# Layer 1 of an LSTM-then-quantum-convolution kernel: results of chunks that lie in the ring go to whole buffers and out from there, and later rows are loaded into the ring

## The chip, the cores and the metric

The kernel runs on one core of a Trainium2 chip. The metric is the device time of one execution in microseconds (us), the median of several. Engines are called as in the profile: PE (TensorE), DVE (VectorE), ACT (ScalarE), POOL (GpSimd), SP (SyncE, which here only issues DMAs). DMAs that SP issues are on queue q1 in the profile, those that POOL issues on q0; all run on the core's 16 DMA engines.

## What is computed

The input is x of 16 images x 128 channels x 64 x 64, in fp32. Two layers, each with a group normalization in front and its result added to x:

```
x = x + diagonal_lstm(group_norm(x))      # layer 0: a scan over 127 diagonals, w_is, w_ss
x = x + quantum_conv(group_norm(x))       # layer 1
...
quantum_conv, for every pixel:
    xq = x[:, pixel] @ pre_w.T + pre_b                     # 128 channels -> 4 angles
    z  = expectation values of a 4-qubit circuit of cos, sin(pi/2 * xq)
    out = z @ post_w.T + post_b                            # 4 -> 128 channels
```

Layer 1 needs the mean and variance of layer 0's whole result, and so begins only when layer 0 is done.

## The kernel before

**Where the data lie.** An image is 128 channels (the partitions) x 4096 pixels, 2 MB. The SBUF tile `ring` (line 109) holds 40 of an image's 64 rows, for all 16 images, as 10 blocks of 4 rows: `ring[P, 10, 16, 256]`. One block of one image is 256 floats, 1 KB in each partition, and the next block of the same image lies 16 KB further on. The other 24 rows, the low ones, have gone to the DRAM tensor `low` (line 112) in the course of layer 0.

**Layer 1** (lines 933 to 1109) works in chunks of 8 rows (`CHUNK`, 512 pixels): 8 chunks an image, of which chunks 0 to 2 (`NT` = 3) are low rows and chunks 3 to 7 are in the ring. A ring chunk is two blocks, so a tensor of three dimensions [128, 2, 256] whose runs are 1 KB; a chunk in a tile of its own is [128, 512] with runs of 2 KB. The low chunks need places in SBUF: `places` (line 944) is first a list of 14 whole tiles, the 8 of `spare` and 6 named `low`. `load(n)` (line 947) takes up to n places from the front of the list and puts the next low chunks of the 48 there, in order of images; the first 8 were loaded by SP at the end of layer 0, all later ones are DMAs issued by POOL (`low_rows`, line 857). `rows_of(b, k)` (line 956) gives chunk k of image b wherever it lies.

For an image there are these steps:
- `angles` (line 971): 8 matmuls, one a chunk, into one PSUM bank (line 976).
- `sines` (line 986): ACT adds the offset (991), DVE takes off whole turns (993, 994), ACT takes the sine (996).
- `squares` (line 998): 2 matmuls (1005) and two squares on ACT (1018).
- `outputs` (line 1020): for each half image h, 4 matmuls (1027) into 4 of 5 PSUM banks, one for each chunk.
- `finish` (line 1037): for each chunk one DVE instruction that adds the bank, a bias and x and writes the sum over x in place (line 1046), then a DMA of it to the output on SP (line 1047); then the place is appended to `places`, so that a later low chunk can be loaded there. Such a load has to wait for the DMA out of the place.

**The order** is written out by hand (`tc.manual_schedule`, lines 1058 to 1109). Image 0 is done in half chunks (argument c is 0 or 1). Then, for image b: outputs of half 0, the first part of the sines of image b+2, finish of half 0, `load(3)`, sine, squares of image b+1, outputs of half 1, finish of half 1, `load(2)`, angles of image b+3. Behind image 0's halves stand `load(3)` (line 1084) and `load(2)` (line 1092). Every engine executes its instructions in this order; so SP's DMAs are in the order of the chunks, and POOL's loads in the order of the low chunks.

Of the kernel before, what the change touches and what calls it, by code (L numbers as in the profile page):

```python
# [11 lines left out]
F32 = mybir.dt.float32  # L12
AF = mybir.ActivationFunctionType
ALU = mybir.AluOpType
PSUM = bass.MemoryType.PSUM

P = 128
NB = 16
NH = 64
# [5 lines left out]
ROWS = 4  # L25
BLOCK = ROWS * NW
CHUNK = 2 * BLOCK
# [53 lines left out]
def kernel(  # L81
# [16 lines left out]
    nc = tc.nc  # L98
# [13 lines left out]
    low = dram.tile([NB, P, NLOW * NW], F32, name="low")  # L112
# [13 lines left out]
    spare = [const.tile([P, CHUNK], F32, name=f"spare{i}") for i in range(8)]  # L126
# [6 lines left out]
    b_out = const.tile([P, 1], F32, name="b_out")  # L133

    def block(r):

        return (r + AHEAD if r < SLOTS else r - SLOTS) // ROWS
# [18 lines left out]
    with ExitStack() as scan:  # L156
# [58 lines left out]
        with ExitStack() as prep:  # L215
# [47 lines left out]
            for i in range(2):  # L263
                nc.scalar.dma_start(out=ws_n[i], in_=ws_v[:, 2 * i : 2 * i + 2])
            nc.scalar.dma_start(
                out=qw, in_=q_weights.rearrange("l w a -> (l w a)").partition_broadcast(P)
# [88 lines left out]
            for i in range(2):  # L355
                v = ws_n[i]
# [500 lines left out]
        def low_rows(queue, n, v):  # L857
            b, k = n // NT, n % NT
            of = low[b, :, k * CHUNK : (k + 1) * CHUNK]
            queue.dma_start(out=v, in_=of if len(v.shape) == 2 else of.rearrange("p (k n) -> p k n", n=BLOCK))  # L860
# [4 lines left out]
        with tc.manual_schedule():  # L865
# [26 lines left out]
            v = ring[:, block(NH - ROWS)].rearrange("p i (r w) -> p i r w", w=NW)[:, :, :, NW - STRIP :]  # L892
# [4 lines left out]
            for i, u in enumerate((d, sq)):  # L897
                u = u.rearrange("p i r w -> p i (r w)")
# [34 lines left out]
    lowp = ctx.enter_context(tc.tile_pool(name="lowp", bufs=1))  # L933
# [7 lines left out]
    ths, turns, sqs = {}, {}, {}  # L941


    places = list(spare) + [lowp.tile([P, CHUNK], F32, name=f"low{i}") for i in range(6)]
    lows = []

    def load(n):

        while n and places and len(lows) < NT * NB:
            v = places.pop(0)  # L950
            lows.append(v)
            if len(lows) > 8:
                low_rows(nc.gpsimd, len(lows) - 1, v)
            n -= 1

    def rows_of(b, k):
        if k < NT:
            return lows[NT * b + k]
        q = block(2 * ROWS * k)
        return ring[:, q : q + 2, b, :]  # L960

    def half(v, c):

        if c is None:
            return v
        return v[:, c] if len(v.shape) == 3 else v[:, c * BLOCK : (c + 1) * BLOCK]

    def bank(pool, name):
        return pool.tile([P, CHUNK], F32, name=name, tag=pool.name)

    def angles(b, c=None, all_of=None):
        th = half(bank(ps_t, f"theta{b}_{c}") if all_of is None else all_of, c)
        for h in range(2):

            for j in (2, 3, 1, 0):
                nc.tensor.matmul(  # L976
                    th[32 * j : 32 * j + 32, :],
                    lhsT=w_image[:, b, 16 - 16 * h : 48 - 16 * h],
                    rhs=half(rows_of(b, 2 * j + h), c),
                    start=(h == 0),  # L980
                    stop=(h == 1),
                    tile_position=(0, 32 * j),
                )
        ths[b, c] = th

    def sines(b, c=None):

        if b not in turns:
            turns[b] = sinp.tile([P, CHUNK], F32, name=f"y{b}", tag="y")
        y = half(turns[b], c)  # L990
        nc.scalar.activation(y, ths[b, c], AF.Identity, bias=b_image[:, b : b + 1])  # L991
        near = half(nearp.tile([P, CHUNK], F32, name=f"near{b}_{c}", tag="near"), c)
        nc.vector.tensor_scalar(near, y, ROUND, ROUND, ALU.add, ALU.subtract)
        nc.vector.tensor_sub(y, y, near)  # L994
        yield
        nc.scalar.activation(y, y, AF.Sin, scale=TWO_PI)

    def squares(b, c=None):
        ams = []
        y = half(turns[b], c)  # L1000
        for h in range(2):
            am = half(ps_a.tile([P, CHUNK], F32, name=f"am{b}_{h}_{c}", tag=f"am{h}"), c)

            k = 64 * h
            nc.tensor.matmul(  # L1005
                am,
                lhsT=w_amp[k : k + 64, h, :],
                rhs=y[k : k + 64, :],
                start=True,
                stop=True,  # L1010
                tile_position=(k, 0),
            )
            ams.append(am)

        if b not in sqs:
            sqs[b] = [sqp.tile([P, CHUNK], F32, name=f"sq{b}", tag="sq"), turns[b]]
        for am, v in zip(ams, sqs[b]):
            nc.scalar.activation(half(v, c), am, AF.Square)

    def outputs(b, h, c=None):  # L1020
        po = [
            half(bank(ps_o, f"po{b}_{h}_{j}_{c}"), c)
            for j in range(4)
        ]
        for j in range(4):
            k = 32 * j
            nc.tensor.matmul(  # L1027
                po[j],
                lhsT=w_out[k : k + 32, :],
                rhs=half(sqs[b][h], c)[k : k + 32, :],  # L1030
                start=True,
                stop=True,
                tile_position=(k, 0),
            )
        return po

    def finish(b, h, po, c=None):
        for j in range(4):
            k = 4 * h + j
            v = rows_of(b, k)  # L1040
            x1, y, o = half(v, c), po[j], ov[b, :, k * CHUNK : (k + 1) * CHUNK]
            if c is not None:
                o = o[:, c * BLOCK : (c + 1) * BLOCK]
            elif len(v.shape) == 3:
                y, o = (u.rearrange("p (k n) -> p k n", n=BLOCK) for u in (y, o))
            nc.vector.scalar_tensor_tensor(x1, y, b_out, x1, ALU.add, ALU.add)  # L1046
            nc.sync.dma_start(out=o, in_=x1)
            if c != 0:
                places.append(v)

    def idle():

        ps = bank(ps_t, nc.get_next_instruction_name())
        v = w_image.rearrange("p b k -> p (b k)")[:, 0:CHUNK]
        for _ in range(2):
            nc.tensor.matmul(ps, lhsT=w_out, rhs=v, start=True, stop=True)  # L1056

    with tc.manual_schedule():
        load(len(places))

        angles(0, 0)
        angles(0, 1, bank(ps_o, "theta0"))
        first = [sines(0, c) for c in range(2)]
        for later in first:
            next(later)

        th = bank(ps_t, "theta1")
        angles(1, 0, th)
        for later in first:
            next(later, None)  # L1070
        squares(0, 0)
        angles(1, 1, th)
        ths[1, None] = th
        po = outputs(0, 0, 0)
        finish(0, 0, po, 0)
        squares(0, 1)
        later = sines(1)
        next(later)
        po = outputs(0, 1, 0)
        finish(0, 1, po, 0)  # L1080
        next(later, None)
        po = outputs(0, 0, 1)
        finish(0, 0, po, 1)
        load(3)
        angles(2)
        later = sines(2)
        next(later)
        po = outputs(0, 1, 1)
        squares(1)
        next(later, None)  # L1090
        finish(0, 1, po, 1)
        load(2)
        angles(3)
        for b in range(1, NB):
            po = outputs(b, 0)
            later = sines(b + 2) if b + 2 < NB else iter(())
            finish(b, 0, po)
            load(3)
            next(later, None)
            if b + 1 < NB:  # L1100
                squares(b + 1)
            next(later, None)
            po = outputs(b, 1)
            finish(b, 1, po)
            load(2)
            if b + 3 < NB:
                angles(b + 3)
            elif b < NB - 1:
                idle()
# [37 lines left out]
```

## Time and profile before

| | |
|---|---|
| median of 3 runs | 1420.79 us (1420.56 to 1421.28) |
| the profiled execution | 1419.29 us |
| its span, first to last instruction | 1417.5 us |
| busy: PE, DVE, POOL, ACT | 95%, 69%, 65%, 55% of the span |
| last instructions of layer 0, first angle matmuls of layer 1 | 1288.3 us after the span's start |
| first result of image 1 on DVE; last result of image 15 | 1305.6; ends at 1399.5 us |
| DVE for a result chunk (line 1046) | 743 ns, one every 0.66 us |
| an image on PE and on DVE, in the middle of layer 1 | 6.33 us |
| DMAs of results of 256 KB: out of ring places, spare, low tiles | 95, 13, 12 |
| loads of low chunks by POOL: to ring places, spare, low tiles | 20, 8, 12 (6 of them first loads) |

The page cuts the span in 40 slices of 35.4 us; its rows give the busy tenths of each engine and of the DMA engines, and the GB/s moved, slice by slice. The other views take a stretch in us from the span's start. In a line of DMA issues the last number is the median time from issue to landing. The DMA share in a table of stretches is the sum of the packets' times over 16 engines' time; packets overlap a little, so that a full stretch has 1.02 to 1.09. Issues on SP are counted as no engine's busy time.

### The profile page before, as it was taken

To read this page: it belongs to the slowest core of one execution; us is meant where nothing else is said; L and a number is where in the kernel's file an instruction comes from. 1 tells how busy PE (TensorE), PEld (TensorE's weight loads), DVE (VectorE), ACT (ScalarE), POOL (GpSimd) and SP (SyncE) were. 2 spreads that over 40 slices of the span, in tenths; PEclk is the share of its full clock that TensorE was granted. 3 is DMA by queue.
4 is the path that set the end of the run, shared out by engine and by line. 5 is a ranking of instruction groups with operands and counts; after the bars stand their busy time and mean duration, and the time that the engine had idled before them with its cause. 6 is when DMAs were issued, how large, how long until landed. Compare 5 with 4: busy or idle time off the path is not lost. (4 is left out here: it accounts for less than half of the span.)

```text
span 1417.5 us, 20294 instructions
## 1 busy us (share of the span) xinstructions
PE 1351.7 (95%) x6030; PEld 962.8 (68%) x6030; DVE 980.5 (69%) x2549; ACT 778.3 (55%) x1860; POOL 923.4 (65%) x1823
## 2 busy tenths in 40 slices
PE   6778999999999999999999999999999999989994
PEld 5658887777777677667777667777777788785331
DVE  7993565566665666787777776766665567867994
ACT  4655666555555555555555555555555556644330
POOL 4226787777766667788888766777777677763400
PEclk9999999999999999999999999999999999999997
DMA  9980000000000000133333100000000000005999
GB/s 325 366 284 2 1 2 0 1 1 1 1 0 1 0 1 1 60 119 119 119 119 119 60 1 1 0 1 1 1 1 0 1 1 0 11 22 193 390 371 323
DMA packets 91086, 107.06 MB, mean 76 GB/s; under 512 B 5552, under 2 KB 78032, under 8 KB 90976
## 3 DMA queue, kind: packets, MB, share of 16 engines
q1 hardware_dynamic: 86336, 94.39, 19.7%
q0 software_dynamic: 3408, 10.58, 2.0%
q8 instruction: 48, 0.79, 0.2%
q10 hardware_dynamic: 1232, 0.80, 0.2%
q14 instruction: 62, 0.51, 0.1%
HBM read 59.61 MB, written 46.14 MB: 75 GB/s over the span
## 5 line engine op out<-in xcount | busy, mean ns | idle before, releaser
L583 PE MATMUL ps<-spare,wxT 128*128 128x512 f32 (+18 forms) x1280 | 479.7, 518 | 0.7 <-POOL spare L574 0.7
L767 DVE TENSOR_TENSOR ps<-ps,both 128x256 f32<-128x256 f32 (+9 forms) x544 | 221.5, 408 | 305.2 <-PE ps L752 303.8
L771 ACT ACTIVATE ps<-ps,bias 128x512 f32<-128x512 f32 (+23 forms) x480 | 279.3, 583 | 220.3 <-DVE ps L767 183.7
L752 PE MATMUL ps<-spare,w1T 128*128 128x256 f32 (+16 forms) x1272 | 345.9, 354 | 9.8 <-DVE spare L729 4.9
L583 PEld LDWEIGHTS ps<-spare,wxT 128*128 128x128 f32 x1280 | 231.1, 190 | 173.1 <-issue 155.4
L752 PE MATMUL ps<-spare,w0T 128*128 128x256 f32 (+16 forms) x1272 | 344.0, 352 | 0.8 <-POOL spare L608 0.8
L802 ACT COPY both<-ps 128x256 f32<-128x256 f32 (+9 forms) x544 | 191.4, 354 | 181.1 <-PE ps L752 161.5
L617 POOL TENSOR_TENSOR ring<-ring,spare 128x256 f32<-128x256 f32 (+8 forms) x487 | 247.3, 538 | 31.3 <-DVE stats L705 21.2
L752 PEld LDWEIGHTS ps<-spare,w1T 128*128 128x128 f32 x1272 | 230.0, 190 | 35.5 <-DVE spare L834 7.6
L752 PEld LDWEIGHTS ps<-spare,wsT 128*128 128x128 f32 x1088 | 195.1, 190 | 86.1 <-DVE spare L834 34.6
L752 PE MATMUL ps<-spare,wsT 128*128 128x256 f32 (+14 forms) x1088 | 241.3, 365 | 5.3 <-DVE spare L834 3.6
L752 PEld LDWEIGHTS ps<-spare,w0T 128*128 128x128 f32 x1272 | 230.5, 190 | 22.0 <-POOL spare L608 0.9
L574 POOL TENSOR_TENSOR spare<-spare,rstd 128x512 f32<-128x512 f32 (+10 forms) x160 | 170.8, 1067 | 14.8 <-DVE rstd L153 2.3
L569 POOL TENSOR_TENSOR spare<-ring 128x256 f32<-128x256 f32 (+8 forms) x213 | 146.8, 699 | 0.0
L828 ACT ACTIVATE g<-cst 128x256 f32<-128x256 f32 (+20 forms) x320 | 103.0, 368 | 64.3 <-DVE cst L827 63.7
L834 DVE TENSOR_TENSOR spare<-g,ps 128x256 f32<-128x256 f32 (+17 forms) x319 | 105.4, 368 | 43.8 <-ACT g L828 41.9
L564 POOL TENSOR_TENSOR spare<-ring,mean 128x16 f32<-128x16 f32 (+8 forms) x247 | 130.6, 538 | 6.6 <-DVE mean L143 6.4
L608 POOL TENSOR_TENSOR spare<-spare 128x240 f32<-128x240 f32 (+9 forms) x136 | 102.6, 754 | 29.7 <-DVE spare L834 25.8
L771 ACT ACTIVATE g<-ps,bias 128x512 f32<-128x512 f32 (+20 forms) x160 | 97.3, 608 | 27.1 <-DVE ps L767 21.1
L854 POOL COPY spare<-spare 128x16 f32<-128x16 f32 x64 | 21.0, 329 | 134.6 <-DVE spare L834 134.6
L827 DVE TENSOR_TENSOR cst<-cst,ps 128x256 f32<-128x256 f32 (+20 forms) x320 | 104.5, 368 | 5.5
L824 DVE TENSOR_TENSOR ps<-ps,g 128x512 f32<-128x512 f32 (+20 forms) x160 | 95.0, 594 | 17.0 <-ACT g L771 16.6
(368 smaller groups left out, 1099.7 us busy)
## 6 DMA issues: line engine op xcount, KB each, us to landing
out_dram<-ring SPq DMA_DIRECT2D x95, 256.0 KB, 3.6
ring<-in_x_dram SPq DMA_DIRECT2D x80, 256.0 KB, 5.6
low<-ring SPq DMA_DIRECT2D x6, 2048.0 KB, 7.5
ring<-in_x_dram SPq DMA_DIRECT2D x6, 2048.0 KB, 8.3
spare<-in_x_dram SPq DMA_DIRECT2D x27, 256.0 KB, 5.5
rest<-in_x_dram SPq DMA_DIRECT2D x21, 256.0 KB, 5.6
ring<-low POOLq DMA_DIRECT2D x20, 256.0 KB, 6.6
out_dram<-spare SPq DMA_DIRECT2D x13, 256.0 KB, 4.0
```

Source lines behind the costliest of these rows:

```text
L564: nc.gpsimd.tensor_sub(by_pairs(xn, 0, j, n), x0, over(mean1, n))
L569: nc.gpsimd.tensor_sub(by_pairs(xn, 1, j, n), lower, of)
L574: nc.gpsimd.tensor_mul(v, v, r)
L583: nc.tensor.matmul(ps[g][:, :, a:b], lhsT=wxT[:, g * 128 : (g + 1) * 128], rhs=xns[t % 2][:, :, a:b], start=t > 0, stop=True, skip_group_c ...
L617: engine.tensor_add(x1, x1, by_pairs(new, q, j, n))
L752: nc.tensor.matmul(out, lhsT=w[:, g * 128 : (g + 1) * 128], rhs=rhs, start=False, stop=True, skip_group_check=True,)
L767: nc.vector.tensor_add(v, v, both[g][:, a:b])
L771: nc.scalar.activation(to[:, :, a:w], ps[g][:, :, a:w], FUNC[g], bias=bias[:, g : g + 1])
L802: nc.scalar.copy(both[g][:, a:b], ps[g][:, 0, a:b])
L827: nc.vector.tensor_add(c[:, q], c[:, q], ig[:, q])
L828: nc.scalar.activation(th[:, q, a:w], c[:, q], AF.Tanh)
L834: nc.vector.tensor_mul(new[:, q, a:v], th[:, q, a:v], act[GO][:, q, a:v])
```

## The change

There are now two lists. `buffers` has the 14 whole tiles; `places` is empty at first, and gets ring places. The first `load` fills all 14 buffers, every later one takes from `places` alone.

```
-    places = list(spare) + [lowp.tile([P, CHUNK], F32, name=f"low{i}") for i in range(6)]
-    lows = []
-
-    def load(n):
+
+    buffers = list(spare) + [lowp.tile([P, CHUNK], F32, name=f"low{i}") for i in range(6)]
+    places, lows = [], []
+
+    def load(n, places=places):
...
             x1, y, o = half(v, c), po[j], ov[b, :, k * CHUNK : (k + 1) * CHUNK]
+            to, short = x1, len(v.shape) == 3
             if c is not None:
                 o = o[:, c * BLOCK : (c + 1) * BLOCK]
-            elif len(v.shape) == 3:
-                y, o = (u.rearrange("p (k n) -> p k n", n=BLOCK) for u in (y, o))
-            nc.vector.scalar_tensor_tensor(x1, y, b_out, x1, ALU.add, ALU.add)
-            nc.sync.dma_start(out=o, in_=x1)
+            elif short:
+                y = y.rearrange("p (k n) -> p k n", n=BLOCK)
+
+                if len(buffers) > NH // ROWS // 2 - 2:
+                    v = buffers.pop(0)
+                    to = v.rearrange("p (k n) -> p k n", n=BLOCK)
+                    places.append(x1)
+                    short = False
+                else:
+                    o = o.rearrange("p (k n) -> p k n", n=BLOCK)
+            nc.vector.scalar_tensor_tensor(to, y, b_out, x1, ALU.add, ALU.add)
+            nc.sync.dma_start(out=o, in_=v if c is None else to)
             if c != 0:
-                places.append(v)
+                (places if short else buffers).append(v)
...
-        load(len(places))
+        load(len(buffers), buffers)
```

In `finish`, a whole chunk that lies in the ring (`short`) is handled in a new way when more than 6 buffers are free: the sum is written to the buffer at the front of the list, the DMA to the output reads the buffer with runs of 2 KB, the ring place is appended to `places` and the buffer to the end of `buffers`. With 6 or fewer free buffers it is written in place and goes out in runs of 1 KB as before. A low chunk in a whole tile is written in place, and its tile then joins `buffers`. A low chunk that was loaded to a ring place is handled like any other ring chunk. Image 0's half chunks are written in place as before. The number of instructions on DVE and of DMAs doesn't change.

## The prediction

> **What bounds the kernel now.** I read the page's slices first, then the chain of waits, then tables by stage, then the DMA view of two stretches. The page (busy tenths and GB/s in 40 slices of 35.4 us):
>
> ```profile
> DVE  7993565566665666787777776766665567867994
> ...
> DMA  9980000000000000133333100000000000005999
> GB/s 325 366 284 2 1 2 0 1 1 1 1 0 1 0 1 1 60 119 119 119 119 119 60 1 1 0 1 1 1 1 0 1 1 0 11 22 193 390 371 323
> ```
>
> Layer 1 is the last four slices; only there are VectorE and the DMA engines both full. Nothing else is touched by the diff, so the question is which of the two sets the end. The chain of waits for 1240 to 1418 ends like this (start, length, what):
>
> ```profile
> 1396.22 1.32 DVE ring L1046 x2
> 1397.53 0.66 DVEq L1143
> 1398.19 1.32 DVE ring L1046 x2
> ```
>
> VectorE's last result is written at 1399.5. The span ends at 1417.5; so 18 us behind the last computation only transfers run. The list for the output tensor gives the last DMA out of the ring at 1412.7, and in this stretch an issue lands after 3.5 us: 1416.2, then 1.3 us of closing. The DMA view of 1306 to 1350 and of 1350 to 1418 (packets, MB, share of 16 engines; then issues):
>
> ```profile
> q1 hardware_dynamic: 7601, 8.80, 56.0%
> q0 software_dynamic: 2498, 8.18, 48.0%
> ...
> out_dram<-ring SPq DMA_DIRECT2D x23, 256.0 KB, 9.1
> ring<-low POOLq DMA_DIRECT2D x19, 256.0 KB, 6.6
> out_dram<-spare SPq DMA_DIRECT2D x8, 256.0 KB, 8.7
> out_dram<-low SPq DMA_DIRECT2D x6, 256.0 KB, 9.5
> ```
>
> ```profile
> DMA packets 22382, 23.23 MB, mean 342 GB/s; under 512 B 1429, under 2 KB 20718, under 8 KB 22376
> ...
> q1 hardware_dynamic: 22365, 23.14, 99.3%
> ```
>
> From 1306 on the 16 engines are never free: first refills (q0) and results (q1) together, then results alone, nearly all in 1 KB packets. By 1350 SP has issued 23 + 8 + 6 = 37 results of images 1 to 15. VectorE, which the chain shows at 6.33 us an image (8 chunks, 0.79 us each) from 1305.6, has written 56. With about 8 of the 37 still in flight (9 us to land, one about every 1.2 us), VectorE leads by some 27 chunks. **The end is set by transfers**, not by VectorE.
>
> **The change, part by part.** (1) *Runs.* Of the 120 chunks of images 1 to 15, 95 go out of ring places now and 25 out of whole tiles (13 spare, 12 low). After it, the five ring chunks of image 1 still go in place (6 free buffers, and the test wants over 6); from image 2 on every chunk goes from a whole tile. So 90 chunks change from 256 x 1 KB to 128 x 2 KB packets. The price of each, from stretches of the table (PE, PEld, DVE, ACT, POOL; last three: clock, DMA share, GB/s):
>
> ```profile
> 1324.00:1328.00 4.00, 4.00 (x24) 1.35 (x22) 3.97 (x8) 1.25 (x3) 2.86 (x5) 1.00 1.08 397
> ...
> 1340.00:1342.00 2.00, 2.00 (x19) 0.42 (x16) 1.97 (x4) 0.69 (x2) 1.73 (x3) 1.00 1.06 413
> 1352.00:1362.00 10.00, 10.00 (x66) 3.17 (x60) 9.93 (x17) 4.30 (x8) 0.00 (x0) 1.00 1.09 381
> ...
> 1378.00:1382.00 4.00, 4.00 (x26) 1.14 (x24) 3.96 (x7) 1.34 (x3) 0.00 (x0) 1.00 1.03 372
> 1382.00:1390.00 8.00, 8.00 (x32) 2.84 (x34) 7.97 (x14) 2.11 (x4) 0.00 (x0) 1.00 1.03 343
> 1400.00:1408.00 8.00, 0.00 (x0) 0.00 (x0) 0.00 (x0) 0.00 (x0) 0.00 (x0) 0.50 1.03 341
> 1410.00:1412.00 2.00, 0.00 (x0) 0.00 (x0) 0.00 (x0) 0.00 (x0) 0.00 (x0) 0.50 1.03 363
> ```
>
> 1382 to 1390 and 1400 to 1408 are pure 1 KB: 342 GB/s, 0.766 us a chunk. 1378 to 1382 holds 686 packets of 1 KB (0.70 MB, 2.05 us at 343) and 384 of 2 KB: these move 0.79 MB in the other 1.95 us, 403 GB/s. 1410 to 1412 by the same sum (267 and 221 packets) gives 377. I take 385 GB/s, between the two, nearer the lower, since no stretch is pure 2 KB. Per packet the DMA views agree: 102.8% of 16 x 8 us over 2680 packets of 1 KB is 48.5 ns after 9 ns for each small one, and the 2 KB ones then have 84 ns, against 97 for two short ones.
> Results alone (1350 to 1416.2, 66.2 us, 23.2 MB, a mean of 350) become 23.2 / 385 = 60.3 us: **minus 5.9 us**. Bounds: 0 (the 1 KB rate of 1352 to 1362, 381, is nearly as good without longer runs) and 23.2 / 403 = 57.6, minus 8.6. With refills beside them, 397 (mostly 1 KB results) and 413 (mostly 2 KB) stand only 4% apart, and part of that stretch is already 2 KB: 17.0 MB at 387 become 17.0 at 395, **minus 0.9 us**; bounds 0 and minus 1.7.
>
> The Trainium skill, "DMA: Bandwidth & Descriptors", speaks against this: under "Specifications" it has 512 B as the least transfer for line rate, and under "Why small descriptors are slow (HBM only)" about 3 cycles on top of each packet's 32-byte beats. By that, at its 850 MHz, 1 KB is an estimated 41 ns and 2 KB 79 ns: 28 ns a chunk, 2.5 us for 90. The trace's 48.5 and 84 ns give 13 ns a pair, 0.10 us a chunk, so I go by the trace.
>
> (2) *Where refills go.* All 34 now go to ring places, instead of 20 ring, 8 spare, 6 low. Issuing costs POOL 0.72 us against 0.55 (line 860 by form): 14 x 0.17 = 2.4 us more on POOL, which does nothing else from 1288 on: nothing on the path. A refill moves in the same large packets either way (8.18 MB in some 2000) and lands after 6.6 against 6.8 us: 0.
>
> (3) *When refills start.* After image 0's first half only its ring place 3 is free for them, so line 1084 asks for 1 row instead of 3, and line 1092 for 2: image 0 ends two rows behind, and stays two behind; the last refill moves from image 6 to image 7. Now three refills are issued at 1301.8 to 1302.9, when the DMA share of 1302 to 1306 is 0.72. Moved behind 1306 they take up to 3 x 0.66 = 2.0 us of a full stretch; some move within free time, so **plus 1.3 us** (0 to 2.0). The rows are needed later: image 4 by the angle matmuls at 1308.9 needs one refill (place 3, whose DMA out landed at 1302.8), image 5 at 1315.2 three. A refill lands 3 to 5 us after issue there, so they are there by about 1311. If not, PE's angle matmuls would wait, and VectorE's lead covers it.
>
> (4) *The ring place is free sooner*, behind VectorE's write instead of behind a landing 9 us later. Refills then follow VectorE. They are 34 all the same, so the engines' work doesn't change: 0.
>
> (5) *The new wait.* Line 1046's successor writes a buffer whose last DMA must have landed. From image 4 on 14 buffers rotate (9 and 12 in images 2 and 3, where the one taken was written at least 12 chunks earlier). VectorE's lead of 27 chunks is cut to 13 or 14. Behind the waiting instruction on VectorE stand the other results of the half image and lines 993 and 994 of image b+2; ACT's sine, then TensorE (five PSUM banks of results) wait for those, SP's issues for the results, POOL's refills for the places. But all of them wait while 13 results stand ready for the DMA engines, 13 x 0.68 = 8.8 us of work. Cost on the path: 0 while VectorE still ends early enough. Check: results landed plus refills landed by 1350 are about 65 now. After it, if VectorE has written n, 13 are under way, and refills landed are 0.625 n - 4: n - 13 + 0.625 n - 4 = 64.5, n = 50 instead of 56. VectorE is 4.7 us late at 1350, and by about 2.5 more when the last six refills are through: 1399.5 + 7.2 = 1406.7, and the last chunk lands some 3 us later, 1409.7. The transfers end later than that, just. So I count 0, with bounds 0 and plus 2.
> The addition itself has the same 128x512 elements and 743 ns, in place or not: 0.
>
> Sum: - 5.9 - 0.9 + 1.3 = - 5.5; with 0.3 for the near tie of (5), **- 5.2 us**. Last landing 1411.0, span 1412.3. The profiled execution took 1419.29 (1.8 around its span) and would take 1414.1; from the median of 1420.79, **1415.6 us**.
>
> **Rivals.** A: as summed, 1412.9 to 1418, chance 0.45.
> B: 2 KB runs go at 403, and the end is VectorE's: with only 5.4 us of waiting it ends at 1404.9, lands at 1407.7, minus 8.5: 1412.3, or little below. For: 403 and 413 in the table. Against: 377. Chance 0.20.
> C: run length doesn't set the rate. For: 1 KB alone went at 381 from 1352 to 1362, when many DMAs stood queued (landing after 4.4 to 5.4 us), and at 342 only when few did (3.5 us). If 350 stays for results alone and only the 0.9 is won, with 1.3 lost: plus 0.4, 1421.2. Against: both 2 KB stretches stand between pure 1 KB ones at 343. Chance 0.20.
> D, slower: VectorE waits for one buffer so long that TensorE runs dry and its clock falls. For: now refills wait for landings, then they don't, and a large refill packet stands between two results. At the end of the record the last matmul ends at 1397.4 and the clock granted is 0.5 from 1399.3: 1.9 us decide. Price: an image of 6.33 us of matmuls takes twice that; two such falls are 12.7, less 5.2 gained: plus 7.5, 1428.3; one is 1421.9. Against: waits come spread, about 0.26 us a chunk, and no earlier idle stretch of TensorE, the longest 1.3 us, cost the clock. Chance 0.15.
>
> A change under 0.2% (2.8 us) can't be told from none here. Faster: B and nearly all of A, 0.64; same: C and the edge of A, 0.21; slower: D, 0.15. The range leaves out the far end of D and a little below B: 1411 to 1421.5.
>
> **What would show it.** Right: packets under 2 KB in the last stretch nearly gone, 375 to 400 GB/s there, VectorE's waits at the results named DMA out_dram, some 5 to 8 us in all, last landing 1411. Wrong: 345 GB/s with 2 KB packets (C), a granted clock under 1 before VectorE's end (D), the DMA share well under 1 in the last 40 us (B).

## The result and the profile after

| | before | after |
|---|---|---|
| median of 12 runs each | 1420.64 us (1418.48 to 1422.88) | 1421.03 us (1418.0 to 1422.74) |
| ratio, 95% interval | | 1.0002 [0.9993, 1.0012] |
| span of the profiled execution | 1417.5 us | 1420.3 us |
| VectorE's last result ends | 1399.5 us | 1416.3 us |
| last DMA lands | 1416.2 us | 1419.05 us |

The time is the same within 0.2%. The forecast of 5.2 us less did not come; 1421.03 us lies within the stated range of 1411 to 1421.5, at its upper end. Line numbers below are those of the kernel after: the result is line 1056 (1046 before), its DMA 1057, a refill 860 as before.

The page's slices of the kernel after (busy tenths, granted clock, DMA share, GB/s):

```profile
DVE  7983555566665666887777776666665567866788
...
PEclk9999999999999999999999999999999999999989
DMA  9980000000000000133333100000000000005998
GB/s 326 369 278 1 1 2 0 1 1 1 1 0 1 0 1 2 60 119 119 119 119 119 60 1 1 0 1 1 1 1 0 2 1 1 31 2 185 390 374 325
```

In the last two slices VectorE has 8 and 8 tenths, where it had 9 and 4; the DMA engines have 9 and 8 (9 and 9 before). They are no longer full at the end; VectorE is, as the table below has it. The last three entries of the chain that ended last say the same (start, length, what); before, 16.7 us of transfers alone stood behind VectorE's end, now 2.7:

```profile
1412.27 2.06 DVE low L1056 x3
1414.33 0.66 DVEq L1153
1414.99 1.32 DVE spare L1056 x2
```

Further up, this chain also names landings of results, some 2 us each. VectorE works 47.0 of the 48 us from 1368 to 1416, so they hold it up by little.

The table by stage shows where VectorE lost its time (PE, PEld, DVE, ACT, POOL busy us and instructions; then granted clock, DMA share, GB/s):

```profile
1298.00:1302.00 4.00, 4.00 (x19) 0.80 (x18) 1.80 (x5) 0.00 (x0) 0.00 (x0) 0.57 0.76 258
1302.00:1306.00 4.00, 4.00 (x36) 1.34 (x36) 2.69 (x6) 2.55 (x5) 0.72 (x1) 1.00 0.37 107
1306.00:1312.00 6.00, 6.00 (x39) 1.84 (x33) 5.24 (x9) 2.21 (x5) 2.85 (x4) 1.00 0.76 217
...
1322.00:1326.00 4.00, 2.04 (x13) 0.34 (x12) 3.95 (x7) 0.81 (x2) 2.49 (x4) 0.93 0.93 280
1326.00:1346.00 20.00, 19.18 (x90) 5.19 (x82) 12.05 (x19) 5.38 (x9) 12.90 (x18) 0.93 1.04 407
1346.00:1354.00 8.00, 7.55 (x13) 2.49 (x14) 3.62 (x6) 1.08 (x2) 1.42 (x2) 0.50 1.04 407
1354.00:1360.00 6.00, 6.00 (x27) 1.11 (x24) 4.18 (x7) 1.32 (x2) 0.00 (x0) 0.54 1.05 405
1360.00:1368.00 8.00, 8.00 (x44) 2.62 (x40) 7.57 (x12) 2.40 (x4) 0.00 (x0) 1.00 1.05 401
1368.00:1392.00 24.00, 24.00 (x141) 7.84 (x140) 23.86 (x39) 9.61 (x16) 0.00 (x0) 1.00 0.88 335
1392.00:1416.00 24.00, 22.19 (x94) 7.40 (x92) 23.13 (x37) 5.21 (x9) 0.00 (x0) 0.96 0.92 350
```

From 1326 to 1360 the DMA engines are full (1.04) while VectorE works 20 of 34 us; from 1368 on VectorE is full and the DMA share is 0.88 to 0.92. Before, VectorE had 19.90 of the 20 us of 1326 to 1346:

```profile
1326.00:1346.00 20.00, 20.00 (x117) 6.69 (x116) 19.90 (x33) 7.91 (x14) 9.72 (x15) 1.00 1.06 402
```

The granted clock was 1.0 throughout layer 1 until 1399.3 before; here it is half in three stretches, 1298.1 to 1301.5, 1325.4 to 1328.9 and 1345.9 to 1359.6 (and from 1414.2 on, at the very end).

Set chunk by chunk against the profile before, VectorE is late as follows:

| until | lateness, us | what stands in front of the step |
|---|---|---|
| start of layer 1 | -0.53 | |
| image 0, second half | 1.11 | half clock: an angle matmul takes 1.07 us instead of 0.62 |
| image 3 | 1.28 | |
| image 4, first result | 5.57 | TensorE waits for a refill |
| image 6, second half | 14.53 | buffers, one after the other |
| image 7 | 16.79 | TensorE still at half clock (2.17 us for one bank) |
| last chunk | 16.8 | nothing more: 6.33 us an image |

The step at image 4 in TensorE's timeline (start, length, idle time before and what ended it):

```profile
1322.57 1.05 PE L977 MATMUL theta_None<-ring,w_image 128*32 128x512 f32 x4
1325.58 3.52 PE L977 MATMUL theta_None<-ring,w_image 128*32 128x512 f32 x12 [1.96 <-DMA ring<-low]
```

The angle matmuls of image 6 stop for a low row that landed at 1325.54. POOL issued it only at 1318.84, as the second of a row of eight that begins at 1318.04, behind 7.19 us of waiting: image 1's ring places still go out in place, and the first of their DMAs landed at 1317.5. The step at images 5 and 6 in VectorE's timeline:

```profile
1343.87 0.75 DVE L1056 SCALAR_TENSOR_TENSOR spare<-po_None,b_out,ring 128x512 f32<-128x512 f32 x1 [0.98 <-DMA out_dram<-spare]
1345.64 0.75 DVE L1056 SCALAR_TENSOR_TENSOR low<-po_None,b_out,ring 128x512 f32<-128x512 f32 x1 [1.02 <-DMA out_dram<-low]
1347.41 0.75 DVE L1056 SCALAR_TENSOR_TENSOR low<-po_None,b_out,ring 128x512 f32<-128x512 f32 x1 [1.02 <-DMA out_dram<-low]
```

A result comes every 1.77 us, where VectorE needs 0.66: each waits for the landing of the DMA that last read its buffer. The DMA view of 1326 to 1346 says why landings are so rare (packets, MB, share of 16 engines; then issues with the median time to landing):

```profile
q0 software_dynamic: 1580, 5.18, 64.7%
q1 hardware_dynamic: 1618, 2.94, 38.6%
...
ring<-low POOLq DMA_DIRECT2D x18, 256.0 KB, 7.8
out_dram<-spare SPq DMA_DIRECT2D x6, 256.0 KB, 14.4
```

The refills (q0) move 5.18 MB, 259 GB/s: one of 262,144 bytes each 1.01 us. That leaves 147 GB/s of the 407 for the results, one each 1.78 us. POOL's speed isn't what sets the 259. It can issue a refill every 0.72 us, as it did eight times from 1318.04 on; later it waits for refills to land:

```profile
1318.04 5.73 POOL L860 DMA_DIRECT2D ring<-low  x8 [7.19 <-DVE spare L1056]
...
1340.55 0.72 POOL L860 DMA_DIRECT2D ring<-low  x1 [1.25 <-DMA ring<-low]
```

In the trace each issue from 1324.59 to 1343.46 begins 0.5 to 0.9 us behind the landing of the refill eight before it, whose semaphore it uses again. At 7.8 us to landing and one each 1.01 us, about eight refills are always under way; so are about eight results (14.4 us, one each 1.78). The DMA engines serve the two queues nearly packet for packet, 1580 against 1618, and a refill's data packets are 4 KB, a result's 2 KB: so the refills get almost twice the bytes. In the same 20 us before, refills moved less and results more, and VectorE, which wrote in place, waited for no landing:

```profile
q1 hardware_dynamic: 3558, 4.16, 57.7%
q0 software_dynamic: 1171, 3.86, 47.7%
```

### The profile page after: what moved, and what is told of

Same layout as the page of the kernel before. It is cut to its first block, busy times and chain, and to the rows that moved or that the text cites. A ratio compares the mean times of both kernels' runs of the same rounds, so it can differ in the third digit from the quotient of the medians.

```text
span 1420.3 us, 20364 instructions
## 1 busy us (share of the span) xinstructions
PE 1363.9 (96%) x6030; PEld 962.6 (68%) x6030; DVE 982.6 (69%) x2549; ACT 777.9 (55%) x1860; POOL 925.2 (65%) x1823
```

## The experiments

The theory I set out with (T): transfers no longer set the end; VectorE does, late by the late refill of image 6 and by waits for buffers while refills take the DMA engines. The rival (R): transfers still set the end, and VectorE's lateness is harmless. A ratio is always to the kernel before on the same chip, with its 95% interval; an ending time is that of the profiled execution. In these executions layer 1 begins anywhere from 1287.8 us (the kernel after) to 1290.5, so ending times alone compare to no better than that.

### Image 1's ring places too go by way of buffers

```
-                if len(buffers) > NH // ROWS // 2 - 2:
+                if len(buffers) > 5:
```

> Theory T (the transfers won what was forecast, but the end is now VectorE's, and VectorE is 16.8 us late: 1.6 at image 0, 4.3 at image 6's late refill, some 11 at buffers and behind them): with image 1's ring chunks in buffers too, the refills of image 6 no longer wait for landings of image 1, the 4.3 us go, but the buffers then run short earlier and take part of it back: 1 to 4 us less than the changed kernel, 1417 to 1420. Rival R (the sum of the transfers still sets the end, VectorE's waits are only its echo): the same time within 1 us, 1420 to 1422.

Measured: 1420.68 against 1421.62 us, 0.9994 [0.9984, 1.0005]. The stop for the late refill is gone, but the waits for buffers now begin at 1322, in image 2, with the same 1.7 us a result; VectorE ends at 1417.1. One wait took the other's place, and the time lies in R's range. In this execution the clock doesn't fall in image 0, and layer 1 begins 2.7 us later than in the kernel after; counted from there, VectorE loses 15.5 us instead of 17.3. The profile speaks for T (VectorE's end and the last landing are 2 to 3 us apart), the time alone for neither.

### The refills' part alone

```
-                if len(buffers) > NH // ROWS // 2 - 2:
+                if len(buffers) > 99:
```

The test is never met: ring chunks are written in place and go out in 1 KB runs, and refills go to ring places.

> Results of ring chunks go out in place in 1 KB runs as before, only the refills go to ring places (the test for free buffers is never met). T: VectorE has no buffer to wait for, the transfers at 342 GB/s set the end, and the later refills add 1 to 3 us to a full stretch: 1421 to 1424. R, and whoever holds that refills into 1 KB runs cost nothing: 1420 to 1421.

Measured: 1423.53 against 1421.62, 1.0016 [1.0008, 1.0025]. Without the 2 KB runs the other parts cost 1.9 us. VectorE ends at 1403.1, and the transfers run on to 1419.4 at the rate of 1 KB runs:

```profile
1400.00:1416.00 16.00, 0.98 (x3) 0.15 (x2) 3.09 (x5) 0.00 (x0) 0.00 (x0) 0.53 1.03 342
```

So moving and delaying refills costs VectorE 3.6 us of its 16.8, 1.6 of them with a fall of the clock in image 0 as in the kernel after; the writing to buffers, and what follows from it, costs the rest. And the 2 KB runs are worth something, since without them the time is longer.

### Fewer refills asked for at each step

```
-            load(3)
+            load(2)
...
-            load(2)
+            load(1)
```

> The changed kernel with three refills an image (2 and 1) instead of five (3 and 2). T: results are no longer crowded out by refills, VectorE waits for buffers 0 to 3 us in all instead of some 9 to 11, image 6's refill is still late by up to 4 us: 1409 to 1415. R: the bytes are the same, so the same time, 1420 to 1422.

Measured: 1419.95 against 1421.62, 0.9993 [0.9984, 1.0002]: a miss for T, and at the edge of R's range. POOL's timeline shows that nothing was slowed:

```profile
1328.11 0.70 POOL L860 DMA_DIRECT2D ring<-low  x1 [0.29 <-issue]
1329.16 0.72 POOL L860 DMA_DIRECT2D ring<-low  x1 [0.34 <-issue]
```

Still one refill a microsecond. POOL executes little else here, and a load takes the oldest place, free for long; its position in the program holds nothing back. Each of these issues again begins 0.5 us behind the landing of the refill eight before.

### Both of these

The edits of the first and the third experiment together.

> Both: image 1's ring chunks in buffers, and three refills an image. T: nearly all of VectorE's lateness goes, its last result ends at 1400 to 1404 and the span 5 us later: 1407 to 1411. R: 1419 to 1422.

Measured: 1420.02 against 1421.62, 0.9989 [0.9981, 0.9998]: a miss for T too, within R's range. VectorE ends at 1415.9. Here VectorE works 18.19 us of 1326 to 1346, but it was 7.5 us late by image 3 already, and from 1338 to 1350 the refills go at 243 to 263 GB/s once more.

The next four go by a sharper theory, T2: refills that run ahead of VectorE crowd the results out, so pacing them by VectorE's own progress brings the gain. Its rival, R2: the time goes with the halved clock or the lists as such, whenever refills come.

### Refills held back by the place that they take

```
-            v = places.pop(0)
+            v = places.pop(0 if places is buffers or len(lows) < 32 else -1)
...
-                if len(buffers) > NH // ROWS // 2 - 2:
+                if len(buffers) > 5:
...
-            load(3)
+            load(3 if b < 4 else 2)
...
-            load(2)
+            load(2 if b < 4 else 1)
```

From the 33rd row on a load takes the newest place, so that POOL has to wait for VectorE.

> Image 1's ring chunks in buffers; five refills an image up to image 3, then three, and each of these goes to the place that came free last, so that it really waits for VectorE's pace (with the oldest place the refills ran ahead one every 1.0 us, whatever their number in the program). Theory T2 (refills that run ahead of need take the DMA engines from the results, these land one every 1.8 us instead of 0.8, VectorE waits for buffers, TensorE thins out and its clock is halved): results land as fast as VectorE writes, waits for buffers under 3 us in all, the clock stays full from image 3 on, last result written by 1400 to 1405: 1405 to 1411. Rival R2 (VectorE's lateness comes from the clock and the two lists as such, not from the pace of the refills): 1418 to 1421.

Measured: 1417.98 against 1421.11, 0.9975 [0.9965, 0.9984]. Just at the edge of R2's range, far from T2's. But the middle of layer 1 is as T2 wants it:

```profile
1312.00:1322.00 10.00, 8.10 (x37) 3.43 (x36) 6.61 (x12) 2.40 (x4) 3.69 (x6) 0.84 0.97 341
1322.00:1326.00 4.00, 4.00 (x19) 0.60 (x16) 3.25 (x5) 0.63 (x1) 2.99 (x5) 0.54 1.05 402
1326.00:1346.00 20.00, 20.00 (x119) 6.65 (x116) 18.62 (x30) 7.89 (x13) 6.06 (x9) 1.00 1.04 397
...
1368.00:1392.00 24.00, 24.00 (x133) 7.72 (x136) 22.94 (x37) 8.79 (x15) 1.38 (x2) 1.00 1.05 404
```

VectorE works 18.62 of the 20 us instead of 12.05, the clock stays full, and 2 KB results move at 404 GB/s. But above it VectorE has lost 9 us by image 3: a fall of the clock in image 0, a wait of 3.33 us at 1318.17 for a buffer of image 1 that had only just been used, and a second fall behind that wait. It ends at 1411.9.

### The newest place, without fewer loads

The same without the two edits of `load`.

> As paced, but still five refills an image. T2: refills follow VectorE at 5 a 6.33 us at most, 0.8 instead of 1.0 a us, so half the crowding: 1411 to 1418. R2: 1418 to 1421.

Measured: 1417.70 against 1421.11, 0.9977 [0.9967, 0.9987], in T2's range at its upper end. The order of places brings in time what it brings together with fewer loads; the same kernel with the oldest place, the first experiment, had 0.9994. The profiled execution is no picture of this gain: at 1420.90 us it is one of the slowest of the nine, with three falls of the clock before VectorE's end at 1415.5.

### The clock kept up by idle matmuls

```
             load(2)
+            if 3 <= b < 7:
+                idle()
             if b + 3 < NB:
```

Two matmuls without use stand in front of the angles of images 6 to 9.

> The changed kernel with a pair of matmuls that nothing needs ahead of the angles behind images 3 to 6, to keep TensorE from thinning out while VectorE waits for buffers. If the halved clock is a cause by itself (R2): VectorE's last result 3 to 6 us earlier, 1414 to 1417. T2 (the clock follows the waits, and costs only the 2 to 3 us after the last of them): 1418 to 1421.

Measured: 1422.61 against 1421.11, 1.0015 [1.0006, 1.0024], worse than either theory had it. The clock still fell (1342.7 to 1349.6, for 6.9 us instead of 13.7) and VectorE ended at 1416.5. Half of the long fall is gone and VectorE is as late as without the idle matmuls, so in these images the halved clock isn't what sets VectorE's end. Why the time is longer isn't shown.

### Eleven buffers instead of fourteen

```
-                    v = buffers.pop(0)
+                    v = buffers.pop(3 if len(buffers) > 13 else 0)
```

> The changed kernel, but from the time that 14 buffers are free the fourth is taken, not the first, so that 11 rotate. T2: VectorE may lead the landings by three chunks less when the refills end, and everything behind is VectorE's: 3 x 0.65 to 0.79, so 2 to 2.4 us more, 1422.5 to 1424.5. If the transfers set the end: 1420 to 1422.

Measured: 1421.84 against 1421.11, 1.0005 [0.9996, 1.0014]. VectorE ends at 1417.6 instead of 1416.3: the sign that T2 wants, but the time lies in the range given for an end set by the transfers, and can't be told from no change. It may be that three buffers more or less only move the moment at which waiting begins; no run shows it. More than 14 were not tried.

### Image 0's places first

```
-                (places if short else buffers).append(v)
+                (places if short or c is not None else buffers).append(v)
```

The whole tiles of image 0's low rows take refills too, so that as many are issued early as before the change.

> The changed kernel, but image 0's three whole tiles take refills once more, as before the change, and join the buffers only after these rows are done; so the refills stand where they stood before, and image 2 goes out in place as well (6 free buffers). If the late refill of image 6 costs what its stop of VectorE lasted (4.3 us), and the end is VectorE's: 2 to 4 us less than the changed kernel, 1417 to 1419. If the lateness is made up for by the waits for buffers behind it, as when image 1 went to buffers: 1420 to 1421.

Measured: 1419.02 against 1420.63, 0.9988 [0.9979, 0.9997], at the upper end of the first range. The late refill of image 6 is gone, the waits for buffers are not; VectorE ends at 1415.5.

### A pair of idle matmuls in image 0

```
         next(later, None)
+        idle()
         po = outputs(0, 0, 1)
```

It fills the 1.04 us for which TensorE waits for free banks there.

> The changed kernel with one pair of matmuls that nothing needs in image 0, in the gap of 1.0 us that TensorE has at 1296. If that gap is what halves the clock at 1298 (in the profiled execution from 1298.1 to 1301.5, VectorE 1.6 us late behind it): the clock stays full there, 1 to 2 us less, 1419 to 1420. If not: 1420.5 to 1421.5.

Measured: 1417.89 against 1420.63, 0.9980 [0.9971, 0.9988], more than expected. The clock stays full until 1336, and the stop at image 6's angles doesn't occur either:

```profile
1298.00:1302.00 4.00, 4.00 (x28) 1.43 (x26) 3.87 (x9) 0.63 (x1) 0.00 (x0) 1.00 0.60 201
...
1326.00:1346.00 20.00, 18.86 (x59) 4.97 (x61) 11.98 (x19) 4.12 (x7) 10.21 (x15) 0.75 1.04 405
```

So the late refill seems to have been in part a consequence of the first fall. The crowding of 1326 to 1346 is still there: VectorE works 11.98 us, almost as in the kernel after. Counted from the start of layer 1, VectorE loses 11.8 us instead of 17.3, and it ends at 1412.8.

### The same pair in the kernel before

> The kernel before with the same pair of matmuls in image 0's gap as idle_image0. If the transfers set the end there (342 GB/s, VectorE 16 us ahead), TensorE's clock at image 0 can cost next to nothing: 1419.5 to 1421, against a gain of about 3 us by the same pair in the changed kernel. If a halved clock at image 0 costs both kernels the same: 1417 to 1418.5.

Measured: 1419.34 against 1420.59, 0.9992 [0.9982, 1.0001], just below what was expected if transfers set the end, and above the other range. In the changed kernel the pair moved the ratio from 1.0002 to 0.9980, some 3.1 us; here by 1.1, not to be told from none. That is for T: computation counts in the changed kernel, and hardly in the one before. It is weaker than I meant it, since in the profiled executions of before the clock was full in image 0 with and without the pair (VectorE ends at 1399.6 and 1399.5).

### All that helped, together

The places of image 0 first, the newest place from the 33rd row on with the two smaller loads, and the idle pair; the test stays at over 6 buffers.

> Refills paced as in paced, image 0's tiles taking refills as in early_first, the pair of matmuls of idle_image0, the test for over 6 free buffers as in the change. If the three delays found (clock at image 0 with 1.6 to 2.9 us, buffers or a late refill at images 2 to 6 with 4 to 5, results crowded out with up to 11) add up: VectorE's last result by 1403 to 1407, 1409 to 1414. If the transfers, short of work before 1312, set a floor: 1414 to 1417.

Measured: 1414.98 (1414.25 to 1417.71, five runs) against 1420.63, 0.9962 [0.9947, 0.9977]. This beats both kernels, the one before by 0.38% or 5.4 us. It lies in the upper of the two ranges. VectorE ends at 1407.7, the last DMA lands at 1411.2; from 1368 to 1392 both VectorE (23.90 of 24 us) and the DMA engines (1.05) are full, so which of them sets the end now is open.

```profile
1326.00:1346.00 20.00, 19.71 (x78) 5.88 (x78) 13.61 (x21) 5.88 (x10) 7.77 (x11) 0.83 1.04 399
...
1368.00:1392.00 24.00, 24.00 (x143) 7.89 (x132) 23.90 (x39) 9.10 (x16) 0.00 (x0) 1.00 1.05 404
1392.00:1416.00 24.00, 13.54 (x52) 4.61 (x46) 14.83 (x23) 2.22 (x5) 0.00 (x0) 0.86 0.73 281
```

DMA view of 1326 to 1346: refills now take 42.1% of the engines and results 61.8%, the reverse of the kernel after, and a result lands after 7.1 us instead of 14.4:

```profile
q1 hardware_dynamic: 2633, 4.73, 61.8%
q0 software_dynamic: 995, 3.23, 42.1%
...
out_dram<-spare SPq DMA_DIRECT2D x11, 256.0 KB, 7.1
```

VectorE still waits 5.7 us for buffers:

```profile
DVE spare L1056 <- DMA out_dram<-spare: 3.4, 3, 1.3
DVE low L1056 <- DMA out_dram<-low: 2.3, 3, 1.0
```

and is 8.2 us late, with one fall of the clock, 1332.5 to 1339.4, in the midst of these waits.

## Why the forecast failed, step by step

That the time lies within the range is luck. The range reached up to 1421.5 for rivals C and D, of which C is refuted below and D came true in part only; the 5.2 us of the forecast didn't come. The time stayed as it was because two things happen to cancel: the transfers need less time than before, but VectorE, 16.8 us late, now ends at 1416.3, where the transfers ended before (1416.2).

**What bounds the kernel now**: right. In the kernel before transfers set the end; the idle pair that quickens only computation brings about 1 us there, not to be told from none.

**(1) Runs**: right in kind, and more than I took. Between 1354 and the end no packet of 1 KB is left, those under 2 KB being the same as those under 512 B:

```profile
DMA packets 12547, 22.89 MB, mean 342 GB/s; under 512 B 1402, under 2 KB 1402, under 8 KB 12540
```

Where the DMA engines are full, results alone go at 401 and 405 GB/s, and 404 in the two kernels held back, where I took 385 with 403 as the bound. At 404, 23.2 MB would take 57.4 us, 8.8 less than before. The kernel after doesn't have it: its mean over this stretch is 342, because the DMA engines wait for VectorE.

**(2) Where refills go**: not tested by itself; the issues take 0.70 to 0.72 us, as worked out. "A refill moves in the same large packets either way" was right, but not its 0: I didn't ask how many refills would then be under way at once. About eight are, and their large packets take 259 GB/s beside the results.

**(3) When refills start**: mis-sized. The DMA share of 1302 to 1306 is 0.37 (0.72 before), of 1306 to 1312 0.76 (1.02), of 1322 to 1326 0.93 (1.06): 1.4 + 1.6 + 0.5 = 3.5 us of the engines' time, part of it for the fallen clock, against plus 1.3. "They are there by about 1311" was worked out for images 4 and 5 only: a refill of image 6 came at 1325, and TensorE and then VectorE lost 4.3 us. "VectorE's lead covers it" was no help, since that lead is what step 5 spends.

**(4) The ring place is free sooner**: this is the step that failed. "Refills then follow VectorE. They are 34 all the same, so the engines' work doesn't change: 0." The work doesn't change, its order does. The wait for a landing was what held refills to the results' own rate: a refill could start only when a result had gone (in the trace of the kernel before, each one from 1316.4 on begins 0.55 to 0.76 us behind a result's landing). With that wait gone, and the oldest free place taken first, refills didn't follow VectorE: they ran one each 1.01 us, held back only by the landing of the refill eight before, while VectorE got one result out each 1.77 us. Taking the newest place, which does make them follow VectorE, moved the ratio from 0.9994 to 0.9977.

**(5) The new wait**: its mechanism was right, its size not. I expected 50 results written at 1350, by holding the refills to 0.625 for each result; there were 40, and 31.8 refills had moved where that rule gives 0.625 x 40 - 4 = 21. So VectorE is 16.8 us late and not 7.2; "the transfers end later than that, just" doesn't hold, and the last landing is 8.05 us behind the 1411.0 of the forecast. The waits named DMA out_dram are only 3.7 + 2.0 us in all, within the 5 to 8 that I gave as a sign of being right. They were a poor sign: the rest of the lateness stands under TensorE's name, for one wait of VectorE holds back the sines and banks that TensorE and ACT need:

```profile
DVE spare L1056 <- PE po_None L1028: 5.9, 5, 2.2
DVE low L1056 <- PE po_None L1028: 4.2, 1, 4.2
DVE spare L1056 <- DMA out_dram<-spare: 3.7, 4, 1.2
...
DVE low L1056 <- DMA out_dram<-low: 2.0, 2, 1.0
```

**Rival B** (2 KB at 403, the end VectorE's) had both halves right and the wrong lateness, 5.4 us. **Rival C** is refuted: 1 KB runs alone went at 342 again in the refills' part alone, 2 KB runs at 401 to 405. (Beside the 381 that 1 KB runs reached from 1352 to 1362 before, the gain is 6% only; why they were quicker there stays open.) **Rival D** happened, in part: three falls of the clock. Its price of 6.33 us for each was too high for the one that stands by itself, in image 0, which cost 1.64; "no earlier idle stretch of TensorE, the longest 1.3 us, cost the clock" was no protection. So the gain at hand went into a new wait: the transfers could have ended earlier, and the end passed to VectorE, 9.6 us later than I had allowed for.

**Not settled**: why the clock falls in image 0 after the change and not before it. The gap is 1.04 us in both, 1296.08 to 1297.12 after and 1296.61 to 1297.65 before. Chance has a part: with image 0 as in the kernel after, the clock fell there for 3.4 or 6.9 us in eight profiled executions, and not at all in that of the first experiment. No run limits how many refills are under way, which would test their part directly. Nor is it settled how the 8.2 us that VectorE is late in the best kernel divide between waits for buffers and the clock that falls among them.

## What to carry to other kernels

A wait that you remove may be the brake that shared an engine out: before taking it away, ask how many transfers the freed queue will then keep under way and how large their packets are, and what that leaves the others. Where a queue must be paced, make it wait for the consumer's progress (the newest place, not the oldest); asking for less at a step of the program does nothing if the places were free long ago. And when a transfer-bound stretch gets quicker, size the next bound, VectorE's lateness here, by the bandwidth left in each stretch and not by a mean over all.

## What the runs showed of the hardware

- Run length matters for stores to DRAM even above 512 bytes: results alone move at 342 GB/s with 1 KB runs (48.5 ns a packet; 381 GB/s in one stretch) and at 401 to 405 with 2 KB (84 ns).
- With both queues full, refills in their larger packets took 64.7% of the engines and results 38.6%. The Trainium skill, "DMA: Bandwidth & Descriptors", "Queues, rings and completion order", says that each engine goes round the queues that have work, a packet at a time. The trace agrees: 1580 packets of refills against 1618 of results in 20 us, so that the queue with the 4 KB packets got 259 GB/s and the one with 2 KB 147.
- TensorE's clock was halved for 3.4, 3.5 and 13.7 us in the kernel after, for 6.9 in others, each about a multiple of 3.4, and this behind gaps of 1.04, 1.96 and (the longest fall) some 0.6 us only. The Trainium skill, "TensorE: Matmul & The Clock Gate", "What's actually happening", has a free-running window of about 3.4 us and the half rate after one idle window. The lengths agree; that a whole window has to be idle does not, by these gaps. A window that runs by its own count could explain why the same gap, 0.5 us earlier, cost the clock in one kernel and not in the other, and why it differs between executions; no run here was made for that.
